# Checking and factoring FFN weights beside attention: sums on VectorE, checks in place, quarters copied DRAM to DRAM, weights fetched an item ahead

## The chip, the cores and the metric

The kernel runs on one core of a Trainium2 chip. The metric is the device time of one execution in microseconds. Three runs of the kernel before gave 885.43, 882.48 and 884.47 us, median 884.47. The engines are called as in the profile: PE is TensorE, PEld its weight load, DVE is VectorE, ACT is ScalarE, POOL is GpSimd and SP is SyncE, which here only issues DMAs.

## What is computed

`x` is (2, 2048, 256) in float32. The result is `x` plus causal attention plus a feed-forward network (FFN), both of the layernormed `x`:

```python
xn = layernorm(x)
q, k, v = xn @ Wq, xn @ Wk, xn @ Wv
attn = softmax(causal(q @ k.T) / 16) @ v @ Wo
tlin = lambda t, w, s: (t @ w.T) * s          # w holds only -1, 0 and 1
h = silu(tlin(xn, w1, s1)) * tlin(xn, w2, s2) # 256 -> 1024
h = gelu(tlin(h, h1, t1))                     # 1024 -> 1024
h = gelu(tlin(h, h2, t2))                     # 1024 -> 1024
out = x + attn + tlin(h, w3, s3)              # 1024 -> 256
```

The weights that setup_inputs makes are ternary, but the kernel does not take this for granted. It looks at them on the chip while attention runs and then branches.

## The kernel before, in words

**Stages.** Attention comes first (to about 285.6 us of the profiled execution), then the FFN (to about 875 us). Rows of `x` are worked in 8 blocks of 512 (4 to each batch). Every operand of attention's matmuls is held as a rounded high part and a low part, `hi` cast by ACT and `lo = src - hi` by DVE (`hi_lo`, L214 and L215).

**Attention.** `start_keys` normalizes a block (DVE statistics L238 and L239, ACT's square root L243, POOL's multiply and add L283). For the first batch PE transposes it (`ptx`, L309), for the second it goes through DRAM (`turn_keys`, L301 to L303). `weights_product` multiplies the weights ahead (`wqk` from `raw_q` and `raw_k`, `wvo` from `raw_v` and `raw_o`; L223 and L228). `score` (L349) makes one row tile of scores: matmuls L364, mask L370, eviction by DVE with a running maximum (L373), Exp by ACT (L385). Weights of the softmax have to be transposed for the next product. `turn_blocks` transposes 32 x 32 blocks on DVE and stores them to DRAM (`d`, L260), `fetch_blocks` reads them back in four quarters in the right order (`e`, L267), both on SP's queue. `turn` (L409) then casts `hi` by ACT (L423) and subtracts `lo` (L425) on POOL for odd blocks and on DVE for even ones. `weigh` (L434) multiplies by v (L443 and L448), scales (ACT L458, DVE L462) and stores `r_d` (L467).

**The work on FFN weights beside it.** One list, `looks` (L506), holds pairs of a gap and a function. `beside(cost)` is called for every piece of attention with the piece's cost in PE columns. From step 3 on it takes the next function off the list once the columns since the last one reach the gap (L574 to L579). The tiles are fetched by DMAs on ACT's queue into `stgp`, a pool of two buffers of 128 x 1024 (L160). There are three kinds of items:

- `look` (w1, w2 and w3): POOL rounds a copy for the FFN (L131), DVE masks the low bits (L526), ACT sums them up (L528).
- `look_signs` (h2) calls `compare`: ACT writes Sign of the tile into a half of `sums` (L537), DVE compares the tile with it (`not_equal`, L539) and accumulates the differences.
- `look_and_factor` (h1): two fetches, two `compare`s, and then, since the FFN multiplies h1 and h2 by a scheme of seven products of half matrices, the sums of half tiles that the scheme needs. `sums_of_factors` makes four (L150, POOL), two at a time. `store_factors` writes them to DRAM in one DMA of 1 MB and the three plain quarters in three DMAs of 256 KB from the staged tiles (L153 to L156, all on SP's queue).

`sums` is the memory of `xh0`, the FFN's first input, which is loaded from `xT_d[0]` at the end of attention (L669). So `compare` and `sums_of_factors` write the same tile:

```python
sign = sums[:, ts(i, 2), :].rearrange("p a o -> p (a o)")
nc.scalar.activation(sign, t, AF.Sign)
nc.vector.scalar_tensor_tensor(
    sign, t, 1.0, sign.bitcast(F32), ALU.mult, ALU.not_equal, accum_out=seen())
```

When the list is empty, DVE reduces all the results (L663), PE sums them over partitions (`pf`, L665) and DVE writes `flag` (L666). Every engine loads the flag at the end of attention (L1028) and branches to `ffn_ternary` or to a general FFN (L1029).

**FFN.** `ffn_ternary` works on pairs of blocks: `first` (w1 and w2, matmuls L715, evictions ACT L720 and DVE L721, splits L698 and L699, sums L741 and L742), the products with h1 and h2 (L763), and w3 (L871). `make_h2` uses `sums_of_factors` and `store_factors` as well, for h2, inside the FFN.

**What sets the order.** The program text is not the order of the queues. The whole is built with a scheduler that orders the instructions of each engine by their dependencies. `tc.issue_after(marks[..])` keeps a look behind the last score eviction (on DVE) or the last Exp (on ACT) that was written before it. DMAs on the queues of SP and ACT signal their landing on eight shared semaphores, handed out in turn, so a DMA can wait for the older one that had its semaphore.

Of the kernel before, what the change touches and what calls it, by code (L numbers as in the profile page):

```python
# [9 lines left out]
F32 = mybir.dt.float32  # L10
# [3 lines left out]
U32 = mybir.dt.uint32  # L14
AF = mybir.ActivationFunctionType
ALU = mybir.AluOpType
# [4 lines left out]
P = 128  # L21
# [18 lines left out]
LOW_BITS = 0xFFF  # L40
# [22 lines left out]
def attn_ffn_kernel(  # L63
# [35 lines left out]
    nc = tc.nc  # L99
    B, S, D = x.shape  # L100
# [4 lines left out]
    HC = H // P  # L105
    SC = 1024
# [14 lines left out]
    HB = H // 2  # L121
    HK = HC // 2
    factors = {k: dram.tile([P, len(STEPS), HK, HB], F32, name=f"factors_{k}") for k in ("h1", "h2")}
# [5 lines left out]
    def rounded(dst, src):  # L129

        nc.gpsimd.tensor_scalar(dst, src, 1.0, 0.0, ALU.mult, ALU.add)  # L131
# [4 lines left out]
    def rows(n, t):  # L136
        return ds((n % NB) * TB + t * P, P)

    def sums_of_factors(sums, halves, which):

        (a11, a21), (a12, a22) = ((t[:, :HB], t[:, HB:]) for t in halves)
        done = sums.bitcast(F32) if sums.dtype == F32R else sums
        for i in which:
            x, y, op = (
                (a21, a22, ALU.add),
                (done[:, 0, :], a11, ALU.subtract),
                (a12, done[:, 1, :], ALU.subtract),
                (a11, a21, ALU.subtract),
            )[i]
            nc.gpsimd.tensor_tensor(sums[:, i, :], x, y, op)  # L150

    def store_factors(f, c, sums, halves):
        nc.sync.dma_start(out=f[:, 1:5, c, :], in_=sums)  # L153
        nc.sync.dma_start(out=f[:, 0, c, :], in_=halves[0][:, :HB])
        for i in range(2):
            nc.sync.dma_start(out=f[:, 5 + i, c, :], in_=halves[1][:, ts(i, HB)])  # L156

    with ExitStack() as actx:
        cp = actx.enter_context(tc.tile_pool(name="cp", bufs=1))
        stgp = actx.enter_context(tc.tile_pool(name="stgp", bufs=2))  # L160
# [186 lines left out]
        marks = {}  # L347
# [122 lines left out]
        def score_steps(n, t):  # L470
            order = list(range(n - n % NB, n + 1))
            return [
                (6 * (TB if m < n else (t + 1) * P), lambda m=m: score(n, t, m, order))
                for m in order
            ]
# [29 lines left out]
        looked = [0]  # L505
        looks = []  # L506

        def seen():
            looked[0] += 1
            return low_bits[:, looked[0] - 1 : looked[0]]  # L510

        def fetched_weights(src, into):
            t = stgp.tile([P, SC], F32, tag="stg", name=f"stg_{len(looks)}_{looked[0]}")
            nc.scalar.dma_start(out=t, in_=src)
            into.append(t)

        def look(src, dst):
            got = []

            def bits():  # L520
                (t,) = got
                if dst is not None:
                    rounded(dst, t)
                tb = t.bitcast(U32)
                with tc.issue_after(marks["DVE"]):
                    nc.vector.tensor_scalar(tb, tb, LOW_BITS, None, ALU.bitwise_and)  # L526
                with tc.issue_after(marks["ACT"]):
                    nc.scalar.activation(t, tb, AF.Copy, accum_out=seen())  # L528

            looks.extend([(6000, lambda: fetched_weights(src, got)), (9000, bits)])  # L530

        sums = xh0.rearrange("p c h t -> p (c h) t")

        def compare(t, i):
            sign = sums[:, ts(i, 2), :].rearrange("p a o -> p (a o)")
            with tc.issue_after(marks["ACT"]):
                nc.scalar.activation(sign, t, AF.Sign)  # L537
            with tc.issue_after(marks["DVE"]):
                nc.vector.scalar_tensor_tensor(  # L539
                    sign, t, 1.0, sign.bitcast(F32), ALU.mult, ALU.not_equal, accum_out=seen()  # L540
                )

        def look_signs(src):
            got = []
            looks.extend([
                (6000, lambda: fetched_weights(src, got)),
                (9000, lambda: compare(got[0], looked[0] % 2)),
            ])

        def look_and_factor(src, f, c):  # L550
            got = []
            looks.extend([
                (6000, lambda: fetched_weights(src[:, c, :], got)),
                (2000, lambda: fetched_weights(src[:, c + HK, :], got)),
                (8000, lambda: compare(got[0], 0)),
                (2500, lambda: compare(got[1], 1)),
                (3500, lambda: sums_of_factors(sums, got, (0, 1))),
                (4000, lambda: sums_of_factors(sums, got, (2, 3))),
                (4000, lambda: store_factors(f, c, sums.bitcast(F32), got)),
            ])  # L560

        for src, dst in ((w1, w1_sb), (w2, w2_sb)):
            for c in range(src.shape[1]):
                look(src[:, c, :], dst[:, c, :])
        for c in range(HK):
            look_and_factor(h1, factors["h1"], c)
            for k in (2 * c, 2 * c + 1):
                look_signs(h2[:, k, :])
        for c in range(0, HC, SC // D):
            look(w3[:, c : c + SC // D, :].rearrange("p c d -> p (c d)"), None)  # L570

        since = [0]

# [28 lines left out]
        tiles = [divmod(i, NT) for i in range(NB * NT - 1, -1, -1)]  # L602
# [39 lines left out]
        while until < len(tiles) - 1:  # L642
# [7 lines left out]
            a = []  # L650
            if j < len(tiles):
                a = score_steps(*tiles[j])
                if j == 0:
                    a = []
            a = a + extra.get(j, [])
# [15 lines left out]
    def ffn_ternary(actx):  # L671
# [154 lines left out]
        def make_h2(c):  # L826
            halves = []
            for k in (c, c + HK):
                t = stgp.tile([P, SC], F32, tag="stg", name=f"stgt_h2_{k}")
                nc.sync.dma_start(out=t, in_=h2[:, k, :])  # L830
                halves.append(t)
            sums = stgp.tile([P, 4, HB], F32, tag="sums", name=f"sums_h2_{c}", bufs=1)
            sums_of_factors(sums, halves, range(4))
            store_factors(factors["h2"], c, sums, halves)
# [240 lines left out]
```

## Time and profile before

| quantity | value |
|---|---|
| median of three runs | 884.47 us (882.48 to 885.43) |
| profiled execution | 885.32 us, of it the span 883.4 us |
| PE busy | 855.4 us (97%) |
| DVE, ACT, POOL busy | 621.6, 498.1, 258.4 us |
| SP's DMA queue, ACT's DMA queue | 149.07 MB, 12.58 MB |
| sums on POOL in attention (L150) | 16, of 1290 to 1524 ns mean by kind |
| Sign on ACT (L537), compare on DVE (L539) | 16 each, 1054 and 1374 ns mean |
| factor stores, h1: 1 MB; 256 KB | 4 landing in 8.6 us; 12 landing in 3.6 us (medians) |
| fetch of weights (512 KB, h1 and h2) | 16 landing in 6.3 us (median) |

A line of the engine timelines reads: start in the span, duration of the group, engine, line, operation, output and inputs, shape, how many, and in brackets the idle time of the engine just before with what ended it. Neighbouring instructions of one line are drawn together, so a group may overlap the next by a pipelined instruction. The number after a line's xcount in the page's groups is busy time and mean duration.

### The profile page before, as it was taken

Reading aid. Unit: us, or ns where it says so; the run is one execution under the profiler, and the core shown is the slowest. Engines: PE = TensorE matmul, PEld = TensorE weight load, DVE = VectorE, ACT = ScalarE, POOL = GpSimd, SP = SyncE. Lnnn points to the kernel's source line nnn. Section 1 sums busy time; section 2 is a strip of 40 time slices with the busy share of each in tenths; the row PEclk is TensorE's granted clock in tenths of the full one; section 3 lists DMA queues with packets and bytes.
Section 4 is the critical chain, followed back from the end, with each engine's and each line's share of the span. In section 5 each row is a group of like instructions: output and inputs, shape, how many; then the busy total and the mean of one; then the engine's idle time right before and its main releaser. Section 6 shows DMA issues by size and latency. Waiting matters only on the chain.

```text
span 883.4 us, 12258 instructions
## 1 busy us (share of the span) xinstructions
PE 855.4 (97%) x4280; PEld 721.5 (82%) x4280; DVE 621.6 (70%) x1111; ACT 498.1 (56%) x881; POOL 258.4 (29%) x192
## 2 busy tenths in 40 slices
PE   8999889999998999999999999999999999999996
PEld 5988678888887878788988888888888898888886
DVE  6698667787763896786497596559568648848663
ACT  3456545755544655677256576626657635657670
POOL 4012835323211384440133051024115011502401
PEclk9999999999999999999999999999999999999999
DMA  8676699987882979844434444433444443144412
GB/s 268 243 224 200 195 313 298 343 298 207 294 253 58 377 256 343 294 143 143 137 102 144 143 143 144 155 109 118 143 142 144 143 144 96 48 143 144 143 48 76
DMA packets 63989, 162.51 MB, mean 184 GB/s; under 512 B 6704, under 2 KB 36528, under 8 KB 54704
## 3 DMA queue, kind: packets, MB, share of 16 engines
q1 hardware_dynamic: 60176, 149.07, 50.3%
q10 hardware_dynamic: 3744, 12.58, 5.0%
q8 instruction: 36, 0.59, 0.3%
q14 instruction: 33, 0.27, 0.1%
HBM read 113.92 MB, written 47.71 MB: 183 GB/s over the span
## 4 chain that ended last, share of the span: by engine, by line
PE 61%; DMA 4%; DVE 1%; POOL 1%; issue 0%; SPq 0%; POOLq 0%; DVEq 0%
PE ps_h_X L763 26%; PE ps_h_Z L763 13%; PE ps_w_B L715 10%; PE ps_h_Y L763 7%; PE ps_y L871 6%; DMA xt<-in_attn_x 2%; DMA w_h_A<-factors_h 1%; POOL rt L861 1%; DMA rt<-r_d 0%; DVE f_w_B L742 0%; DVE h_B L699 0%; POOL f_w_B L741 0%; DMA out<-yt 0%; DVE yt L878 0%; DVE yt L877 0%
## 5 line engine op out<-in xcount | busy, mean ns | idle before, releaser
L364 PE MATMUL pss<-k,q 128*128 128x512 f32 (+3 forms) x480 | 109.6, 369 | 3.7 <-ACT q L214 2.4
L364 PEld LDWEIGHTS pss<-k,q 128*128 128x128 f32 x480 | 82.3, 190 | 17.2 <-ACT q L214 2.7
L763 PE MATMUL ps_h_X<-h_h_T,w_h_S 128*128 128x512 f32 x384 | 89.0, 389 | 0.0
L443 PE MATMUL po<-v,pT 128*128 128x512 f32 x272 | 80.4, 407 | 6.5 <-ACT pT L423 5.8
L763 PEld LDWEIGHTS ps_h_X<-h_h_T,w_h_S 128*128 128x128 f32 x384 | 72.1, 188 | 15.0
L861 POOL TENSOR_TENSOR rt<-rt,xt 128x1024 f32<-128x1024 f32 x8 | 19.2, 2400 | 218.7 <-DMA rt<-r_d 212.1
L425 POOL TENSOR_TENSOR pT<-e,pT 128x512 fp32r<-128x512 f32 (+3 forms) x30 | 36.9, 1230 | 116.5 <-ACT pT L423 78.7
L784 ACT ACTIVATE k_h_u<-k_h_u,h_s_sb 128x512 f32<-128x512 f32 x64 | 46.3, 723 | 40.9 <-DVE k_h_u L783 40.7
L720 ACT ACTIVATE f_w_B<-ps_w_B,w_s_sb 128x512 f32<-128x512 f32 x64 | 43.0, 684 | 42.5 <-PE ps_w_B L715 42.5
L871 PEld LDWEIGHTS ps_y<-w_sbt,h_h_B 128*128 128x128 f32 x512 | 62.0, 192 | 0.3
L871 PE MATMUL ps_y<-w_sbt,h_h_B 128*128 128x256 f32 x512 | 62.1, 283 | 0.0
L715 PE MATMUL ps_w_B<-xh,w_sb 128*128 128x512 f32 x256 | 59.7, 390 | 1.3 <-DVE r L462 1.3
L715 PE MATMUL ps_w_B<-xh1t,w_sb 128*128 128x512 f32 x256 | 60.7, 397 | 0.0
L443 PEld LDWEIGHTS po<-v,pT 128*128 128x128 f32 x272 | 48.1, 192 | 15.0 <-ACT pT L423 6.7
L763 PE MATMUL ps_h_Y<-h_h_B,w_h_A 128*128 128x512 f32 x256 | 59.5, 389 | 0.6 <-DMA w_h_A<-factors_h 0.6
L763 PE MATMUL ps_h_X<-h_h_T,w_h_A 128*128 128x512 f32 x256 | 59.3, 389 | 0.0
L715 PEld LDWEIGHTS ps_w_B<-xh1t,w_sb 128*128 128x128 f32 x256 | 48.1, 188 | 12.0 <-ACT f_w_B L720 0.4
L715 PEld LDWEIGHTS ps_w_B<-xh,w_sb 128*128 128x128 f32 x256 | 47.8, 188 | 11.4 <-issue 1.5
L763 PEld LDWEIGHTS ps_h_Y<-h_h_B,w_h_A 128*128 128x128 f32 x256 | 48.0, 188 | 10.9 <-issue 1.0
L741 POOL TENSOR_TENSOR k_h_u<-k_h_p,k_h_u 128x512 f32<-128x512 f32 x16 | 24.3, 1526 | 110.0 <-ACT h_h_B L698 97.6
L763 PEld LDWEIGHTS ps_h_X<-h_h_T,w_h_A 128*128 128x128 f32 x256 | 48.1, 188 | 10.0
L385 ACT ACTIVATE s<-s,low 128x1024 f32<-128x1024 f32 (+7 forms) x48 | 43.0, 897 | 21.9 <-DVE low L379 21.8
(139 smaller groups left out, 1869.9 us busy)
## 6 DMA issues: line engine op xcount, KB each, us to landing
w_h_S<-factors_h SPq DMA_DIRECT2D x32, 1024.0 KB, 4.8
w_h_A<-factors_h SPq DMA_DIRECT2D x24, 1024.0 KB, 4.9
d<-b SPq DMA_DIRECT2D x18, 512.0 KB, 3.5
e<-d SPq DMA_DIRECT2D x72, 128.0 KB, 4.0
xT_d<-k SPq DMA_DIRECT2D x8, 1024.0 KB, 5.3
stg<-in_ffn_h_w ACTq DMA_DIRECT2D x16, 512.0 KB, 6.3
x<-in_attn_x SPq DMA_DIRECT2D x16, 256.0 KB, 5.3
r_d<-r SPq DMA_DIRECT2D x8, 512.0 KB, 5.8
```

Of the source, the lines that this page charges most:

```text
L364: nc.tensor.matmul(out=ps[:, :w], lhsT=qs[n][:, c, a, ts(t, P)], rhs=ks[m][:, c, b, :w], start=(k == 0), stop=(m < n and k == 3 * DC - 1),)
L385: marks["ACT"] = nc.scalar.activation(st["s"][:, at], st["s"][:, at], AF.Exp, bias=low, accum_out=st["sums"][:, u // UK : u // UK + 1],).ins
L425: engine.tensor_tensor(lo, src, hi.bitcast(F32), ALU.subtract)
L443: nc.tensor.matmul(out=st["po"], lhsT=pT[:, 0, ts(j, P)], rhs=vs[m][:, j, :, :], start=(m == first and j == 0), stop=False,)
L715: nc.tensor.matmul(out=p, lhsT=w[:, c, ts(o, P)], rhs=xh[:, c, a, :], start=(c == 0 and a == 0), stop=(c == DC - 1 and a == 1),)
L720: nc.scalar.activation(f, p1, AF.Silu, scale=sc["w1"][:, o : o + 1])
L741: nc.gpsimd.tensor_tensor(B["B12"][i], B["B22"][i], B["B12"][i], ALU.subtract)
L763: nc.tensor.matmul(out=out[o], lhsT=w[:, c, ts(o, P)], rhs=sets[right][c][:, a, :], start=(start and c == 0 and a == 0), stop=(c == HK - 1 ...
L784: nc.scalar.activation(C[k][o], r[o] if r else banks[o], AF.Gelu, scale=s[:, at : at + 1])
L861: nc.gpsimd.tensor_tensor(rest, rest, xt, ALU.add)
L871: nc.tensor.matmul(out=ys[t][:, :D], lhsT=h[c][:, a, ts(t, P)], rhs=w3_sb[:, c, :], start=(c == 0 and a == 0), stop=(c == HC - 1 and a == 1),)
```

## The change

- `sums_of_factors` takes the engine as an argument. For h1 in attention it is DVE, and the four sums of an item are four entries of the list, each kept behind the last score eviction. In the FFN it stays on POOL.
- The ternary check of h1 and h2 (`odd`) works in the staged tile: ACT writes the tile's absolute value over it, and DVE computes `(t != 0) != t` in place, accumulating. `sums` is no longer written by checks.
- The sums of an h1 item now come ahead of its checks, as the checks destroy the tile.
- The three plain quarters of h1 are copied from the input in DRAM to `factors` in DRAM by three DMAs on ACT's queue, in place of three stores from the staged tiles on SP's. The 1 MB store of the sums stays on SP.
- Items stand in one list with their sources. An item is fetched ahead of the work on the one before it where both fit in the pool's two buffers. The gaps are new. The two w3 items are interleaved with h1's items 2 and 3.

In the built program the order of the queues follows from these and from the scheduler. The twelve copies read only inputs, and they stand near the head of ACT's queue: three ahead of the first square root, two ahead of `wf_wqk`, three ahead of the third square root, one ahead of the cast of `q_3`, one ahead of the fourth square root and two ahead of `wf_wvo`. The last item of h1 and the three items after it stand in attention's last part, and the flag is made ahead of the products for the last row tile but one. The order of the FFN is almost that of before.

```diff
--- before.py
+++ after.py
@@ -136,7 +136,7 @@
     def rows(n, t):
         return ds((n % NB) * TB + t * P, P)
 
-    def sums_of_factors(sums, halves, which):
+    def sums_of_factors(sums, halves, which, engine=nc.gpsimd):
 
         (a11, a21), (a12, a22) = ((t[:, :HB], t[:, HB:]) for t in halves)
         done = sums.bitcast(F32) if sums.dtype == F32R else sums
@@ -147,7 +147,7 @@
                 (a12, done[:, 1, :], ALU.subtract),
                 (a11, a21, ALU.subtract),
             )[i]
-            nc.gpsimd.tensor_tensor(sums[:, i, :], x, y, op)
+            engine.tensor_tensor(sums[:, i, :], x, y, op)
 
     def store_factors(f, c, sums, halves):
         nc.sync.dma_start(out=f[:, 1:5, c, :], in_=sums)
@@ -509,65 +509,91 @@
             looked[0] += 1
             return low_bits[:, looked[0] - 1 : looked[0]]
 
-        def fetched_weights(src, into):
-            t = stgp.tile([P, SC], F32, tag="stg", name=f"stg_{len(looks)}_{looked[0]}")
-            nc.scalar.dma_start(out=t, in_=src)
-            into.append(t)
-
-        def look(src, dst):
-            got = []
-
-            def bits():
-                (t,) = got
-                if dst is not None:
-                    rounded(dst, t)
-                tb = t.bitcast(U32)
-                with tc.issue_after(marks["DVE"]):
-                    nc.vector.tensor_scalar(tb, tb, LOW_BITS, None, ALU.bitwise_and)
-                with tc.issue_after(marks["ACT"]):
-                    nc.scalar.activation(t, tb, AF.Copy, accum_out=seen())
-
-            looks.extend([(6000, lambda: fetched_weights(src, got)), (9000, bits)])
-
-        sums = xh0.rearrange("p c h t -> p (c h) t")
-
-        def compare(t, i):
-            sign = sums[:, ts(i, 2), :].rearrange("p a o -> p (a o)")
+
+        items = []
+
+        def low(tiles, dst):
+            (t,) = tiles
+            if dst is not None:
+                rounded(dst, t)
+            tb = t.bitcast(U32)
+            with tc.issue_after(marks["DVE"]):
+                nc.vector.tensor_scalar(tb, tb, LOW_BITS, None, ALU.bitwise_and)
             with tc.issue_after(marks["ACT"]):
-                nc.scalar.activation(sign, t, AF.Sign)
+                nc.scalar.activation(t, tb, AF.Copy, accum_out=seen())
+
+        def odd(t):
+
+            with tc.issue_after(marks["ACT"]):
+                nc.scalar.activation(t, t, AF.Abs)
             with tc.issue_after(marks["DVE"]):
                 nc.vector.scalar_tensor_tensor(
-                    sign, t, 1.0, sign.bitcast(F32), ALU.mult, ALU.not_equal, accum_out=seen()
-                )
-
-        def look_signs(src):
-            got = []
-            looks.extend([
-                (6000, lambda: fetched_weights(src, got)),
-                (9000, lambda: compare(got[0], looked[0] % 2)),
-            ])
-
-        def look_and_factor(src, f, c):
-            got = []
-            looks.extend([
-                (6000, lambda: fetched_weights(src[:, c, :], got)),
-                (2000, lambda: fetched_weights(src[:, c + HK, :], got)),
-                (8000, lambda: compare(got[0], 0)),
-                (2500, lambda: compare(got[1], 1)),
-                (3500, lambda: sums_of_factors(sums, got, (0, 1))),
-                (4000, lambda: sums_of_factors(sums, got, (2, 3))),
-                (4000, lambda: store_factors(f, c, sums.bitcast(F32), got)),
-            ])
+                    t, t, 0.0, t, ALU.not_equal, ALU.not_equal, accum_out=seen()
+                )
+
+        sums = xh0.rearrange("p c h t -> p (c h) t")
+
+        def sum_up(tiles, i):
+            with tc.issue_after(marks["DVE"]):
+                sums_of_factors(sums, tiles, (i,), nc.vector)
+
+        def store_sums(f, c):
+            nc.sync.dma_start(out=f[:, 1:5, c, :], in_=sums.bitcast(F32))
+
+        def copy_factors(src, f, c):
+            nc.scalar.dma_start(out=f[:, 0, c, :], in_=src[:, c, :HB])
+            for i in range(2):
+                nc.scalar.dma_start(out=f[:, 5 + i, c, :], in_=src[:, c + HK, ts(i, HB)])
+
+        def item_low(src, dst):
+            items.append(([src], [(0, lambda t: low(t, dst))]))
+
+        def item_signs(src):
+            items.append(([src], [(0, lambda t: odd(t[0]))]))
+
+        def item_factors(src, f, c):
+            steps = [(0, lambda t: sum_up(t, 0))]
+            steps += [(2500, lambda t, i=i: sum_up(t, i)) for i in (1, 2, 3)]
+            steps += [
+                (1500, lambda t: store_sums(f, c)),
+                (1500, lambda t: odd(t[0])),
+                (3000, lambda t: odd(t[1])),
+                (3000, lambda t: copy_factors(src, f, c)),
+            ]
+            items.append(([src[:, c, :], src[:, c + HK, :]], steps))
 
         for src, dst in ((w1, w1_sb), (w2, w2_sb)):
             for c in range(src.shape[1]):
-                look(src[:, c, :], dst[:, c, :])
+                item_low(src[:, c, :], dst[:, c, :])
+        w3_at = list(range(0, HC, SC // D))
         for c in range(HK):
-            look_and_factor(h1, factors["h1"], c)
+            item_factors(h1, factors["h1"], c)
             for k in (2 * c, 2 * c + 1):
-                look_signs(h2[:, k, :])
-        for c in range(0, HC, SC // D):
-            look(w3[:, c : c + SC // D, :].rearrange("p c d -> p (c d)"), None)
+                item_signs(h2[:, k, :])
+            if c >= 2:
+                w = w3_at[c - 2]
+                item_low(w3[:, w : w + SC // D, :].rearrange("p c d -> p (c d)"), None)
+
+        def fetched_weights(i):
+            for src in items[i][0]:
+                t = stgp.tile([P, SC], F32, tag="stg", name=f"stg_{i}_{len(tiles_of[i])}")
+                nc.scalar.dma_start(out=t, in_=src)
+                tiles_of[i].append(t)
+
+
+
+        tiles_of = [[] for _ in items]
+        looks = [(0, lambda: fetched_weights(0))]
+        for i, (srcs, steps) in enumerate(items):
+            nxt = i + 1 < len(items) and len(srcs) + len(items[i + 1][0]) <= 2
+            if nxt:
+                looks.append((4000, lambda i=i: fetched_weights(i + 1)))
+            ahead = i > 0 and len(srcs) + len(items[i - 1][0]) <= 2
+            gap = (8000 if ahead else 11000) if nxt else 15000
+            looks.append((gap, lambda i=i, f=steps[0][1]: f(tiles_of[i])))
+            looks += [(gap, lambda i=i, f=f: f(tiles_of[i])) for gap, f in steps[1:]]
+            if not nxt and i + 1 < len(items):
+                looks.append((4000, lambda i=i: fetched_weights(i + 1)))
 
         since = [0]
 
```

## The prediction

> **What bounds the kernel now.** I read the busy line of the page first, then the TensorE timeline with its idle times, then what the other engines did at those moments, and last the stretches of 20 us.
>
> ```profile
> PE 855.4 (97%) x4280; PEld 721.5 (82%) x4280; DVE 621.6 (70%) x1111; ACT 498.1 (56%) x881; POOL 258.4 (29%) x192
> ```
>
> TensorE is busy 855.4 of 883.4 us, so 28 us is all that any change which leaves the matmuls alone can win. About 8 us of that lies behind the last matmul and 2.8 us in the FFN (2.19 us at 317.80, 0.61 us at 354.97). The rest is in attention. These are its large gaps on the TensorE timeline (start, duration, group, idle time before it and what ended it):
>
> ```profile
> 9.43 2.09 PE L309 MATMUL ptx<-ident,x 128*128 128x128 f32 x8 [1.24 <-POOL x L283]
> ...
> 106.66 1.19 PE L443 MATMUL po<-v,pT 128*128 128x512 f32 x4 [1.35 <-ACT pT L423]
> 109.10 0.74 PE L448 MATMUL po<-v,pT 128*128 128x256 f32 x4 [1.25 <-DVE pT L425]
> ...
> 128.29 1.22 PE L364 MATMUL pss<-k,q 128*128 128x512 f32 x2 [2.36 <-ACT q L214]
> 129.31 1.91 PE L443 MATMUL po<-v,pT 128*128 128x512 f32 x4
> ...
> 267.80 1.70 PE L443 MATMUL po<-v,pT 128*128 128x512 f32 x4 [3.36 <-ACT pT L423]
> ```
>
> Four gaps of over 1 us stand beside work of FFN weights or behind a fetch of scores. After the 2.36 us gap four L443 matmuls take 1.91 us; with no gap before them the same four take 1.09. In the stretches of 20 us (columns: stretch, length, busy time of PE, PEld, DVE, ACT and POOL, PEclk, DMA share, GB/s) see PE's time and PEclk:
>
> ```profile
> 0.00:20.00 20.00, 16.35 (x60) 9.91 (x61) 12.58 (x52) 6.51 (x14) 10.61 (x28) 0.91 0.79 254
> 20.00:40.00 20.00, 20.00 (x144) 18.67 (x143) 11.41 (x25) 9.05 (x15) 2.10 (x2) 1.00 0.79 279
> 100.00:120.00 20.00, 17.41 (x98) 14.89 (x98) 16.87 (x43) 13.29 (x25) 10.27 (x8) 1.00 1.01 282
> 120.00:140.00 20.00, 17.64 (x93) 15.20 (x92) 11.41 (x29) 10.58 (x20) 3.80 (x4) 0.91 1.02 317
> 260.00:280.00 20.00, 16.64 (x90) 14.25 (x89) 7.61 (x20) 8.49 (x17) 4.31 (x4) 0.91 0.40 120
> ```
>
> What the neighbours did at 106 to 109 and at 125 us, from the timelines of VectorE, GpSimd and ScalarE:
>
> ```profile
> 106.14 1.22 DVE L539 SCALAR_TENSOR_TENSOR xh<-stg,xh 128x1024 fp32r<-128x1024 f32 x1
> ...
> 107.29 1.76 DVE L425 TENSOR_TENSOR pT<-e,pT 128x512 fp32r<-128x512 f32 x1
> ```
> ```profile
> 108.45 1.74 POOL L150 TENSOR_TENSOR xh<-stg,xh 128x512 fp32r<-128x512 f32 x1
> ```
> ```profile
> 125.39 2.00 ACT L537 ACTIVATE xh<-stg 128x1024 fp32r<-128x1024 f32 x2 [1.30 <-DMA factors_h<-xh]
> ...
> 127.66 0.57 ACT L214 CAST q<-pq 128x512 fp32r<-128x512 f32 x1
> ```
>
> So the 1.25 us gap is a subtraction (L425) behind a check (L539), and the subtraction took 1.76 us beside GpSimd's sum where it takes 0.69 alone. The 2.36 us gap is a cast of q that stood behind two Signs, which had themselves waited 1.30 us until the store of the last sums had read `xh`, because Sign writes where the sums lie.
>
> **What the Trainium skill says.** "SBUF — State Buffer", section "Who interferes with whom": only the port pair shared by VectorE and GpSimd contends, as an exclusive lock. The trace agrees: L425 at 1.76 against 0.69 us, L539 at 2.24 (97.88 us, beside GpSimd's L425) against 1.22. "DMA: Bandwidth & Descriptors", section "Queues, rings and completion order": each DMA engine goes round between the queues that have work. The trace of before has two such queues, SP's and ACT's, and no copy from DRAM to DRAM, nor does the page price one. "TensorE: Matmul & The Clock Gate", section "Part 1: The HAM clock gate": recent idleness throttles the clock. The trace agrees (1.91 against 1.09, and PEclk 0.91 in the two stretches with the longest gaps).
>
> **The change, part by part.**
>
> *Sums from GpSimd to VectorE.* GpSimd loses 16 sums, four each of 1295, 1524, 1521 and 1290 ns, 22.5 us. VectorE gains 16 tensor_tensors of 128x512 with two SBUF operands. The nearest row (L425 on VectorE, alone) is 0.69 us: 11 us. VectorE is busy 16.9 of 20 us in the fullest stretch, with the old checks of 1374 ns mean instead of 1.22: without GpSimd's sums 16 x 0.15 = 2.4 us comes back. Net some 8.6 us more on VectorE over 200 us, no path in the mean, but each sum can stand ahead of a score eviction (L373) or an L425. At TensorE I credit the whole gap at 109.10, 1.25 us.
>
> *Checks in place.* 16 Signs (1054 ns) become 16 Abs of the same shape, 16 not_equals stay not_equals of the same shape; I price the pairs equal. What goes is the wait of Sign for the store: 5.7 us in three places on ScalarE, one of them the cause at 128.29. Credit 2.36 us, and the slow clock after it: four L443 +0.82, six 384-column L364 at 1.59 against 1.20 +0.39, and as much again in the L320 behind, together 1.6 us. At 106.66 a Sign of 1.04 us ran just ahead of the cast for which TensorE waited 1.35: Abs goes elsewhere in ScalarE's order, credit 1.0.
>
> *Copies instead of stores.* SP loses 12 stores of 256 KB from `stg` (L154, L156; 3.6 us each to land) and the waits for `stg` ahead of them (7.5 us at L154). ACT gains 12 issues of 0.33 us, 4 us of its sequencer. In the built order they do not stand where the source has them. They depend on nothing, and all twelve stand at the head of ACT's queue: three ahead of the first square root (`std_3`), two ahead of `wf_wqk`, three ahead of `std_1`, one ahead of the cast of `q_3`, three between it and `wf_wvo`. Nine of them wait for an older DMA, since eight completion semaphores are shared by both queues. So at the start ACT waits for landings, and 3.1 MB more is read and written while 5.07 MB is moved in 20 us at a DMA share of 0.79. The DMA engines reach 380 GB/s in their full slices there: 8.2 MB takes 21.6 us, so the start just holds them if a copy costs what a load costs. `std_3` needs x_3 (its last half arrives at 6.4 us, the first copies are issued at about 1.7 to 2.5 behind raw_q and raw_k): up to 0.3 us late. The k_3 cast at 11.45 stands behind raw_o, which waits for the third copy: with half of 380 GB/s from 5.8 us on (raw_k's landing) three copies of 262 KB need 4.1 us, and land at 10 to 11; raw_o was issued at 10.50 anyway. The cast is late by 0 to 1 us, later ones likewise. I take +1.5 us; bounds 0 and +8.5 (the slower rival). Below zero it can't be: no load is removed there.
>
> *An item fetched ahead, four sums one by one.* Checks no longer wait for their fetch (1.1 us of ScalarE's idle time, off the path). But a fetch into a two-buffer pool waits for the check that frees the buffer, and now does so on ACT's queue: ahead of casts of pT (three times in the last 45 us) with VectorE's check ending just before. Such a stall of about 1 us reaches TensorE where no scores are left to do. New stalls in 100 to 250 us: +2.0 in all; bounds 0 and +5 (five of the size 0.98 at 96.61).
>
> *The tail.* The last checks ran at 250 us; now the last item of h1 and the three after it lie in attention's last 45 us. SP's order changes too. For: the four quarters of the fetch that TensorE waits for at 267.80 are now issued together, and ahead of the store of r_6; before, two stood behind it (the last ten fetches took SP 10.55 us from 260.43), and scores now lie between the products there. Against: the load of `xh` for the FFN now waits on SP until the last 1 MB store of sums has read it (8.6 us to land), and behind it stand the fetches of e_7_1_0. Issued at about 248.4 it lands at 257; those fetches began at 254.4, so 2.6 us late, of which TensorE has 2.8 us of other products to hide in. I credit 1.0 of the 3.36 plus 1.5 us (L443 1.70, L448 1.05 at the slow clock); bounds -4 and +3.
>
> *FFN.* Its order is almost that of before. GpSimd runs four L741 before an L150, where L150 stood ahead of the fourth: this may shorten the 2.19 us at 317.80 (GpSimd's L741 at 317.82 ended 1.68 later). Credit 0.5; bounds 0 and -2.
>
> Sum: -1.25 -2.36 -1.6 -1.0 -1.0 -0.5 +1.5 +2.0 = -4.2 us. Against the profiled execution's 885.32 us (span 883.4, 1.9 around it) that is 881.1. The profiled run lies 0.85 above the median of 884.47, so at the median's level the same sum gives 880.3; I keep 881.1, and judge the cases' sides against the median.
>
> **The rivals.**
>
> *Gaps move (884.0).* The scheduler orders every engine anew, VectorE has 11 us more ahead of evictions, and the 6.2 us of gaps return elsewhere. For: gaps at 96.61 and 153.70 have no look near them. Against: two causes (the wait for a store, the shared port) disappear altogether. New waits then cost 5 instead of 2: 884.1.
>
> *The copies hold ACT's queue at the start (888.1), slower.* If a DRAM-to-DRAM copy runs at half a load's rate, three copies beside SP's loads take 8.3 us, not 4.1: raw_o is issued at 14 to 15, the k_3 cast slips from 11.45 by 3.4 us, and wf_wvo (19.35), behind the twelfth copy, comes at 25 to 28, 6 to 8.5 us late, with v's products and all that follow behind it. Start +8.5 instead of +1.5: 881.1 + 7.0 = 888.1. It decides from a copy rate below about 0.6 of a load's. For: nothing measures it here, and the start has a DMA share of 0.79 already. Against: the copies are behind the first four loads, and TensorE has scores of block 3 in hand at 18 us.
>
> *The tail clears too (875.8).* Whole tail 4.9 instead of 1.0, new waits 0.6 instead of 2.0: 881.1 - 3.9 - 1.4.
>
> **How the numbers follow.** A measurement here tells 0.3%, 2.65 us, from no change. Forecast (877 to 884): 0.45, of which 0.12 lies within 2.65 us. Gaps move: 0.18 (0.04 faster, 0.10 same, 0.04 slower). Copies: 0.25 (0.22 slower, 0.03 same). Tail clears: 0.12. Faster 0.49, same 0.25, slower 0.26. Range 875 to 889: from the tail's case to just above the copies'; since the cases lie on both sides, the forecast's own range stands beside it: 877 to 884.
>
> **What would show it.** Start: first twelve copies on ACT's queue before 20 us; wf_wvo within 2 us of 19.35 (forecast) or past 25 (rival). GpSimd idle of L150 before the FFN, VectorE's L425 at 0.69. No idle time of ScalarE on a store of sums; no 2.36 us gap near 128, PEclk 1.00 there. Tail: the gap at 267.80 under 2.5 us, SP waiting for the last store ahead of `xh`. Wrong if TensorE's idle before 30 us grows by over 3 us, if VectorE's sums end gaps at L364, or if the last 45 us hold more idle than 4.9 us.

## The result, and the profile after

| | before | changed |
|---|---|---|
| median of five executions | 884.47 us (882.48 to 886.63) | 877.43 us (876.67 to 878.56) |
| ratio, 95% interval | | 0.9924 [0.9899, 0.9949] |
| profiled execution (span) | 885.32 (883.4) | 877.43 (875.6) |
| attention ends, first FFN matmul | 285.62 us | 279.72 us |
| last group of matmuls (w3) starts | 859.92 us | 853.02 us |
| span after the last matmul ends | 8.0 us | 7.1 us |

The kernel became 0.76% faster. The forecast was 881.1, so the sign and the range held, and the size was short by 3.7 us. Of these, 0.85 is a matter of level: the forecast was counted down from the profiled 885.32, and the median lies 0.85 lower. Profile against profile, the forecast's sum of -4.2 stands against -7.9. Of the 7.8 us between the two spans, 5.9 had been won by the end of attention, 1.0 more by the last group of matmuls, and 0.9 after it.

The changed kernel's busy line:

```profile
PE 854.3 (98%) x4280; PEld 721.6 (82%) x4280; DVE 630.6 (72%) x1127; ACT 498.0 (57%) x881; POOL 235.6 (27%) x176
```

Its larger gaps on the TensorE timeline:

```profile
9.36 1.52 PE L309 MATMUL ptx<-ident,x 128*128 128x128 f32 x6 [1.62 <-POOL x L283]
...
22.55 0.50 PE L364 MATMUL pss<-k,q 128*128 128x512 f32 x1 [0.63 <-ACT k L214]
...
123.43 0.73 PE L364 MATMUL pss<-k,q 128*128 128x512 f32 x2 [0.44 <-ACT q L214]
125.98 0.50 PE L364 MATMUL pss<-k,q 128*128 128x512 f32 x1 [1.71 <-DVE q L215]
...
215.69 1.20 PE L443 MATMUL po<-v,pT 128*128 128x512 f32 x4 [1.05 <-DVE r L462]
261.27 1.20 PE L443 MATMUL po<-v,pT 128*128 128x512 f32 x4 [1.93 <-ACT pT L423]
263.60 1.22 PE L448 MATMUL po<-v,pT 128*128 128x256 f32 x4 [1.13 <-DVE pT L425]
```

And its stretches (columns as in the prediction):

```profile
0.00:20.00 20.00, 16.30 (x56) 9.82 (x57) 11.89 (x49) 5.24 (x11) 8.70 (x25) 0.83 0.89 297
20.00:40.00 20.00, 19.37 (x142) 17.86 (x141) 12.78 (x26) 8.99 (x16) 3.86 (x6) 1.00 1.03 385
100.00:120.00 20.00, 20.00 (x111) 17.12 (x110) 18.75 (x37) 12.10 (x24) 7.12 (x5) 1.00 1.00 299
120.00:140.00 20.00, 17.85 (x96) 15.27 (x96) 14.61 (x38) 9.84 (x20) 2.57 (x2) 0.91 1.01 296
260.00:280.00 20.00, 16.31 (x85) 13.71 (x86) 9.01 (x17) 8.00 (x16) 3.78 (x3) 0.91 0.19 50
```

Adding up the gaps of each timeline: those before 50 us (without the first 1.19) went from 2.45 to 3.29, those from 50 to 240 us from 8.49 to 3.20, those from 240 us to the FFN from 3.36 to 3.06, those inside the FFN from 2.80 to 2.01 (the 1.28 us ahead of the FFN's first matmul is the same in both). TensorE's busy time fell by 1.1 us besides. Most of the win is in the middle of attention. The start became dearer, and the stretch from 120 to 140 us still holds its gap and its slow clock.

### The profile page after: what moved, and what is told of

Same layout as the page of the kernel before. It is cut to its first block, busy times and chain, and to the rows that moved or that the text cites. A ratio compares the mean times of both kernels' runs of the same rounds, so it can differ in the third digit from the quotient of the medians.

```text
span 875.6 us, 12225 instructions
## 1 busy us (share of the span) xinstructions
PE 854.3 (98%) x4280; PEld 721.6 (82%) x4280; DVE 630.6 (72%) x1127; ACT 498.0 (57%) x881; POOL 235.6 (27%) x176
## 4 chain that ended last, share of the span: by engine, by line
PE 70%; DMA 13%; DVE 7%; issue 2%; ACT 2%; SPq 2%; POOL 2%; ACTq 0%; DVEq 0%; POOLq 0%
PE ps_h_X L789 26%; PE ps_w_B L741 13%; PE ps_h_Z L789 13%; PE ps_h_Y L789 7%; PE ps_y L897 6%; DMA e<-d 6%; DMA d<-b 4%; DMA stg<-in_ffn_h_w 2%; SPq L267 2%; DVE b L255 2%; PE pv L336 1%; PE po L443 1%; DVE stg L530 1%; POOL x L283 1%; DVE s L373 1%
## 5 line engine op out<-in xcount | busy, mean ns | idle before, releaser
L364 PE MATMUL pss<-k,q 128*128 128x512 f32 (+3 forms) x480 | 111.0, 369 | 3.1 <-DVE q L215 1.7
L364 PEld LDWEIGHTS pss<-k,q 128*128 128x128 f32 x480 | 81.8, 189 | 16.2 <-DVE q L215 2.1
L425 POOL TENSOR_TENSOR pT<-e,pT 128x512 fp32r<-128x512 f32 (+3 forms) x30 | 36.3, 1212 | 162.3 <-ACT pT L423 101.6
L423 ACT CAST pT<-e 128x512 fp32r<-128x512 f32 (+3 forms) x60 | 32.6, 573 | 49.6 <-DMA e<-d 38.3
L741 PEld LDWEIGHTS ps_w_B<-xh1t,w_sb 128*128 128x128 f32 x256 | 48.1, 188 | 11.8
```

The source lines that it names most:

```text
L364: nc.tensor.matmul(out=ps[:, :w], lhsT=qs[n][:, c, a, ts(t, P)], rhs=ks[m][:, c, b, :w], start=(k == 0), stop=(m < n and k == 3 * DC - 1),)
L423: nc.scalar.copy(hi, src)
L425: engine.tensor_tensor(lo, src, hi.bitcast(F32), ALU.subtract)
L741: nc.tensor.matmul(out=p, lhsT=w[:, c, ts(o, P)], rhs=xh[:, c, a, :], start=(c == 0 and a == 0), stop=(c == DC - 1 and a == 1),)
```

## The experiments

Twelve kernels ran, in three sets, each with executions of the kernel before beside it (medians 884.70, 884.76 and 885.16); the five executions of the changed kernel stand apart from these sets. The intervals are some 0.2% wide to each side, so smaller differences between two rows are not told apart. Single executions of one kernel spread over several us (52 of the kernel before ran from 880.04 to 889.97), so verdicts go by the ratios, and a profile shows one execution. The last column is TensorE's idle time in the stretch from 90 to 170 us, 80 minus its busy time there.

| kernel | median, us | ratio to before, 95% interval | idle 90 to 170 us |
|---|---|---|---|
| before | 884.47 | 1 | 7.30 |
| changed | 877.43 | 0.9924 [0.9899, 0.9949] | 2.15 |
| b_dve | 882.96 | 0.9974 [0.9955, 0.9993] | 5.03 |
| b_copy | 879.07 | 0.9939 [0.9922, 0.9955] | 5.14 |
| b_inplace | 885.59 | 1.0002 [0.9982, 1.0021] | 9.17 |
| a_tied | 887.02 | 1.0015 [0.9994, 1.0035] | 6.91 |
| a_mid | 880.95 | 0.9953 [0.9936, 0.9971] | 4.17 |
| a_store | 878.95 | 0.9947 [0.9927, 0.9966] | 3.58 |
| a_pool | 880.24 | 0.9954 [0.9938, 0.9969] | 3.56 |
| a_noahead | 878.93 | 0.9940 [0.9922, 0.9957] | 5.61 |
| b_null | 883.31 | 0.9989 [0.9971, 1.0007] | 7.70 |
| a_null | 878.85 | 0.9931 [0.9907, 0.9955] | 4.21 |
| b_poolq | 899.90 | 1.0167 [1.0135, 1.0199] | 13.19 |
| a_poolq | 887.71 | 1.0032 [1.0017, 1.0047] | 5.36 |

The theory at first was that of the prediction: what pays is that look work no longer stands beside attention's casts and subtractions. Its main rival was that SP's queue pays.

### One part alone: b_dve

```diff
-                (3500, lambda: sums_of_factors(sums, got, (0, 1))),
-                (4000, lambda: sums_of_factors(sums, got, (2, 3))),
+                (3500, lambda: sum_up(got, 0)),
+                (2000, lambda: sum_up(got, 1)),
...
+            with tc.issue_after(marks["DVE"]):
+                sums_of_factors(sums, tiles, (i,), nc.vector)
```

> The kernel before with one part alone: h1's four sums per item on VectorE, one by one. Theory (the gain comes from work that stood beside attention's casts and subtractions: the shared port and the wait of Sign for the store of sums): the port is free of GpSimd's sums, so the 1.25 us gap at 109 goes, VectorE pays 15 us in pieces of 0.7 to 1.2: 1 to 3 us faster, 881.5 to 883.5 (median before 884.47). Rival A (the gain comes from SP's queue, which loses twelve stores): no change, 884 to 885. Rival B (a new order of the queues, whatever the part): anything between 880 and 888, with gaps in new places that no row of sums explains.

It gave 0.26% [0.07, 0.45], some 2.3 us: as the theory expected in size, but not in place. The gap at 109 did not go. In b_dve's profile it is 2.05 us, at 111.20, and what stands ahead of the subtraction on VectorE is the check, stretched from 1.22 to 2.32 us:

```profile
108.21 2.32 DVE L539 SCALAR_TENSOR_TENSOR xh<-stg,xh 128x1024 fp32r<-128x1024 f32 x1
...
110.47 0.68 DVE L425 TENSOR_TENSOR pT<-e,pT 128x512 fp32r<-128x512 f32 x1
```

GpSimd ran nothing but attention's own L425 then (1.28 us from 108.17). So GpSimd's sums were not alone in stretching the work of VectorE. In this profile the last matmul ends 4.5 us earlier than in the kernel before (870.97 against 875.43), and 3.7 of them are lost behind it, where 11.7 us pass instead of 8.0. The end of the kernel varies that much, so one profile does not tell what the part is worth.

### One part alone: b_copy

```diff
-                (4000, lambda: store_factors(f, c, sums.bitcast(F32), got)),
+                (4000, lambda: store_and_copy(src, f, c)),
...
+            nc.scalar.dma_start(out=f[:, 0, c, :], in_=src[:, c, :HB])
+            for i in range(2):
+                nc.scalar.dma_start(out=f[:, 5 + i, c, :], in_=src[:, c + HK, ts(i, HB)])
```

> The kernel before with one part alone: the three plain quarters of h1 copied from DRAM to DRAM on ACT's queue, in place of twelve stores on SP's. The copies stand at the head of ACT's queue as in the changed kernel. Theory: the start costs 1.5 to 2 us, SP's relief gives back 0 to 1 us, so 884.5 to 886.5. Rival A (SP's relief is the gain): 3 to 5 us faster, 879.5 to 881.5, with the waits of L423 for e<-d shorter from 90 us on.

0.61% faster, 5.4 us: the rival was right on this part and the theory wrong. The start cost what it costs in the changed kernel (gaps of 3.26 us before 50 us). What came back can be followed at one place. In the kernel before, the store of a plain quarter (L154) stood on SP's queue for 5.3 us, until its tile had landed, and a fetch of scores stood behind it. ScalarE's cast L423 then waited 4.45 us for that fetch, VectorE's subtraction and an eviction (L373) came late after it, and TensorE stood for 0.98 us. The kernel before, on SP's queue (a group's duration holds the waits inside it), ScalarE and TensorE:

```profile
80.91 1.27 SPq L267 DMA_DIRECT2D e<-d  x2
87.52 0.34 SPq L154 DMA_DIRECT2D factors_h<-stg  x1
...
88.43 11.89 SPq L267 DMA_DIRECT2D e<-d  x7
```
```profile
94.02 0.62 ACT L423 CAST pT<-e 128x512 fp32r<-128x512 f32 x1 [4.45 <-DMA e<-d]
```
```profile
96.61 1.66 PE L364 MATMUL pss<-k,q 128*128 128x512 f32 x6 [0.98 <-DVE s L373]
```

And b_copy, SP's queue and ScalarE:

```profile
87.68 12.48 SPq L267 DMA_DIRECT2D e<-d  x9
```
```profile
91.64 0.62 ACT L423 CAST pT<-e 128x512 fp32r<-128x512 f32 x1 [1.34 <-DMA e<-d]
```

The cast runs 2.4 us earlier and TensorE has no gap there. At 45 us it was 1.9 us behind the kernel before, at 96.6 us it is level, and without the gap of 1.35 us at 106.66 it is 1.2 us ahead. This is one place in one profile, and not a rule: b_null keeps the stores, holds SP for 5.0 us at L154 and has no gap near 97. Nor does the sum of such waits tell the gain. Between 30 and 290 us L423 waited 36.3 us for fetches of `e` in the kernel before and 26.8 in b_copy, but 38.3 in the changed kernel, and 20.2 in b_dve and 21.0 in a_store, which leave the stores on SP. So b_copy shows that the edit pays, and for the most of it not by which wait. In the tail the 3.36 us gap became 1.08 and 0.45. The gap of 1.25 us behind VectorE's L425 (107.87) stayed, with L425 at 1.76 us beside GpSimd, as in the kernel before.

### One part alone: b_inplace

```diff
-                nc.scalar.activation(sign, t, AF.Sign)
+                nc.scalar.activation(t, t, AF.Abs)
...
-                    sign, t, 1.0, sign.bitcast(F32), ALU.mult, ALU.not_equal, accum_out=seen()
+                    t, t, 0.0, t, ALU.not_equal, ALU.not_equal, accum_out=seen()
```

The sums and stores of an h1 item also move ahead of its two checks.

> The kernel before with one part alone: checks in place (Abs over the tile, not_equal over it), so that the sums and the stores of an item's quarters come ahead of its checks. Theory: ScalarE no longer waits for the store of sums (5.7 us in three places), so 1 to 3 us faster, 881.5 to 883.5; but Abs on h1's tiles now has to wait until the three 256 KB stores have read them (3.6 us each to land), which may give it all back. Rival A: no change, 884 to 885. If this wait is what the copies are for: slower by 1 to 3 us, 885.5 to 887.5, with L537 waiting for factors_h<-stg.

No change, so the theory missed. The waits for the store of sums are gone from ScalarE, but no wait of Abs for a 256 KB store came instead. Another did: a fetch of weights, held on ScalarE's queue, and behind it stood what TensorE needed. ScalarE:

```profile
148.16 0.33 ACTq L514 DMA_DIRECT2D stg<-in_ffn_h_w  x1
148.60 0.47 ACT L458 ACTIVATE y<-po,inv 128x256 f32<-128x256 f32 x1 [5.36 <-DMA x<-d_x]
...
151.96 1.12 ACT L301 CAST k<-x 128x512 fp32r<-128x512 f32 x2
```

and TensorE:

```profile
152.61 1.22 PE L320 MATMUL pq<-k,wqk 128*128 128x512 f32 x2 [6.44 <-ACT k L301]
```

The scaling L458 does not read `x`. In the built order the fetch ahead of it waits for a completion semaphore that a fetch of `x` on SP's queue had before it. Until that `x` landed, ScalarE stood for 5.36 us and then still had a check to run ahead of the cast of k.

### Where the copies stand: a_tied and a_mid

```diff
+            with tc.issue_after(marks["ACT"]):
+                nc.scalar.dma_start(out=f[:, 0, c, :], in_=src[:, c, :HB])
```

a_tied, in the first set, is this edit for all three copies of an item. After that set theory 2 took the place of the theory: what pays is that the bytes and issues of the quarters leave SP's queue in attention's full stretch. a_mid, in the second set, has the edit too, and calls `copy_factors` for one item at each of steps 1 to 4, not from the list.

> The changed kernel with one edit: each item's three copies are kept behind the last Exp that was written before them, so that they are issued in attention at about 110, 150, 185 and 240 us and not at the head of ACT's queue. Theory (the start costs 1.7 us by the gaps before 46 us): 875.5 to 876.5 against 877.43. Rival C (in attention, where the DMA share is 1.0 from 100 to 160 us, the copies delay the fetches of e and stand in ACT's queue ahead of casts): 878 to 881, and the start's gain is given back.

> The changed kernel with the copies moved on purpose: each item's three copies stand behind an Exp of steps 1 to 4, at about 40 to 60 us, past the crowded start and ahead of the stretch in which the DMA share is 1.0. Theory 2, formed after the last four runs (what pays is that 3.1 MB are no longer moved by SP's queue in the stretch from 100 to 260 us; where they go before it is a matter of the start's 1.7 us): 875 to 877, the start's gaps as in the kernel before. Rival B (each edit draws a new order, and the changed kernel has drawn a good one): 878 to 886, with gaps at new places between 100 and 270 us though the DMA engines are as free there as in the changed kernel.

a_tied lost everything: 887.02 against 877.43, on the side of rival C and past its numbers. Its start is that of the kernel before (gaps of 2.40 us before 50 us), but in attention the queue of ScalarE was held as in b_inplace. ScalarE, then TensorE:

```profile
162.00 0.34 ACTq L581 DMA_DIRECT2D stg<-in_ffn_h_w  x1
162.38 0.47 ACT L458 ACTIVATE y<-po,inv 128x256 f32<-128x256 f32 x1 [3.31 <-DMA factors_h<-xh]
```
```profile
163.43 1.19 PE L443 MATMUL po<-v,pT 128*128 128x512 f32 x4 [2.30 <-DVE r L462]
```

The 1 MB store (issued at 153.91) had the semaphore for which the fetch waits in the built order. The scaling, VectorE's L462 and TensorE stood behind. a_mid, with the copies at 40 to 60 us, kept 0.47%. It missed its forecast of 875 to 877 and lies within the range of its rival B. The start's gaps were saved (1.89 us), but the tail of the profile holds 5.03 us, 3.50 in one gap. So the kernel is slower with the copies in attention's full stretch (0.9% over the changed kernel) than with them at 40 to 60 us (0.3%), and the hoist to the head of the queue, which I had counted as pure cost, is not beaten by either later place. Whether a_tied lost by the copies' bytes or by the waits that they put on ScalarE's queue, these runs do not separate.

### One part taken out: a_store, a_pool, a_noahead

```diff
-                (1500, lambda t: store_sums(f, c)),
+                (1500, lambda t: store_factors(f, c, sums.bitcast(F32), t)),
```
```diff
-                sums_of_factors(sums, tiles, (i,), nc.vector)
+                sums_of_factors(sums, tiles, (i,))
```
```diff
-            nxt = i + 1 < len(items) and len(srcs) + len(items[i + 1][0]) <= 2
+            nxt = False
```

a_store also drops the copies from the list, a_pool the hold of the sums behind the last eviction, and a_noahead has the old gaps (6000 and 9000).

> The changed kernel without its copies: the three quarters are stored from the staged tiles on SP's queue, after the 1 MB store of the sums and ahead of the checks that overwrite the tiles. Theory 2: the gain is gone or turned, since the bytes are back in attention and Abs waits for the stores to have read its tile: 883 to 888. Rival A2 (sums on VectorE and the fetch an item ahead carry the gain, copies not needed): 876 to 879.

> The changed kernel with h1's sums on GpSimd again, still one by one. If VectorE's sums are worth what they gave alone (0.26% of the kernel before, 1 to 4 us by the interval): 878.5 to 881. Rival (with copies out of attention the port matters no more, and VectorE saves 15 us of sums): 876 to 878.

> The changed kernel without the fetch an item ahead, with the gaps of the kernel before (6000 columns ahead of a fetch, 9000 ahead of its work). Fetches no longer stand in ACT's queue behind a check that has to free the buffer, and checks may wait for a fetch (3.5 us in two places now). Expected, as fetches land in 6 us and 9000 columns are about 4.5 us of TensorE: within 2 us of the changed kernel, 876 to 880. Rival B (order): up to 885 with gaps at places that no fetch explains.

Each of the three keeps 0.46 to 0.60%. a_store went against theory 2: without any copy, with the stores on SP in attention, the kernel is still 0.53% faster than before. Abs waited 0.8 us in all for a store that reads its tile. a_pool and a_noahead came as expected. Single parts add up to 0.85% (0.26, 0.61 and -0.02), the whole is 0.76%, and no part that is taken out costs more than 0.3%. This reads as if the parts reach for the same idle time, but it is not shown: the intervals of all three overlap with that of the changed kernel, and a_store and a_noahead (878.95 and 878.93) stand no higher than a_null below (878.85), in which no part is missing. What stays open is how a_store comes by its 0.53%: it has the sums on VectorE, the checks in place behind the stores and the fetch ahead all at once, and no run separates these three from each other in the absence of copies.

### Two controls: b_null and a_null

```diff
-            looks.extend([(6000, lambda: fetched_weights(src, got)), (9000, bits)])
+            looks.extend([(6000, lambda: fetched_weights(src, got)), (8000, bits)])
```
```diff
-        looks = [(0, lambda: fetched_weights(0))]
+        looks = [(4000, lambda: fetched_weights(0))]
```

> A control: the kernel before with one number changed, the gap between a fetch of w1, w2 or w3 and its work, 8000 columns for 9000. No work is removed, added or moved to another engine; later looks come some 1000 columns earlier. Theory 3 (what an edit of the looks gives is for a good part the order that it draws; a fetch of weights on ACT's queue waits for an older DMA that had the same completion semaphore, and casts stand behind it, at places that shift with every edit): the time moves by 1 to 5 us either way, 880 to 888, with the large gaps at other places than before. Theory 2 (the parts themselves carry the gain): 884 to 885.5.

> The same control on the changed kernel: the first fetch comes 4000 columns later and the list with it, nothing else. Theory 3: 877 to 885, with large gaps elsewhere. Theory 2: 877 to 878.5.

Neither control is clear of the kernel that it was made from, so no shift of the order is seen to give anything like the 5 to 7 us of b_copy and the changed kernel. Theory 3 is not refuted for small moves: both medians (1.2 us under that of the kernel before, or 1.9 under that of their set, and 1.4 us over that of the changed kernel) lie in its ranges and just outside those of theory 2. A new order does move the gaps. In b_null's profile one of 5.06 us stands at 132.45, where the kernel before has none, behind a cast that waited 7.80 us for a fetch of scores. SP had drawn out the issues of that fetch and the one before it over 8.19 us. TensorE, then SP's queue:

```profile
132.45 2.08 PE L443 MATMUL po<-v,pT 128*128 128x512 f32 x4 [5.06 <-ACT pT L423]
```
```profile
118.78 8.19 SPq L267 DMA_DIRECT2D e<-d  x8
```

But their sum hardly changes (7.70 against 7.30 us of idle time from 90 to 170 us). In the changed kernel it does: a_null's profile, the slowest of its seven executions, has 4.21 us there against 2.15, and 5.78 against 3.20 from 50 to 240 us. So the place of a gap is drawn anew with each order, and how much of the sum is drawn with it stays open.

### Fetches on GpSimd's queue: b_poolq and a_poolq

```diff
-                nc.scalar.dma_start(out=t, in_=src)
+                nc.gpsimd.dma_start(out=t, in_=src)
```

> The kernel before with the fetches of looks issued by GpSimd's queue in place of ACT's. If casts and scalings that stand behind a waiting fetch on ACT make the gaps, these go: 879 to 882. If instead GpSimd's own waits (L425 stands behind a fetch that waits for its buffer) make new ones, or its issue takes more than ACT's 0.33 us: 884 to 888.

> The changed kernel with the fetches of looks issued by GpSimd's queue, which has lost its sums and so stands idle for longer; the copies stay on ACT's. Theory 3: the stalls of ACT behind fetches go, 875 to 877.5, a little faster than the changed kernel. Else, with new waits of GpSimd's L425 behind fetches that wait for a check: 878 to 882.

Both are slower than the kernel before and past all their forecasts. New waits came on GpSimd in b_poolq (total, times, longest):

```profile
POOL stg L514 <- DVE xh L539: 38.5, 5, 12.6
```

A fetch into a two-buffer pool waits for the check that frees its buffer, and on GpSimd attention's own work then stands behind it. But only one gap of TensorE, 1.07 us, ends with GpSimd's L425. The four gaps over 2 us that b_poolq has in attention (4.41, 5.59, 2.02 and 2.89 us) end with casts of ScalarE. Ahead of the first, at 110.25, a check on ScalarE had waited for a fetch that GpSimd issued only at 101.49, after its own L283 and L425:

```profile
107.51 1.06 ACT L537 ACTIVATE xh<-stg 128x1024 fp32r<-128x1024 f32 x1 [6.07 <-DMA stg<-in_ffn_h_w]
```

So the waits run both ways, and which of them costs the 1.7% is not shown. Taking the shared semaphores from ScalarE was to test the mechanism of b_inplace and a_tied; since another wait took its place, these two runs do not tell how much of the whole it explains.

## Why the prediction was right and where it was short

**Start, +1.5: right.** Gaps before 50 us rose by 0.84 us, PEclk in the first 20 us fell from 0.91 to 0.83, and the group of 24 L364 that begins at 43.93 in the kernel before begins at 45.65, 1.72 later. The gaps are half of it, and the rest goes with the slower clock. Ten of the twelve copies waited for an older DMA, where I had counted nine. The copies cost what loads cost; the issue row and two lines of ScalarE's timeline in the changed kernel:

```profile
factors_h<-in_ffn_h_w ACTq DMA_DIRECT2D x12, 256.0 KB, 5.8
```
```profile
20.97 0.38 ACT L228 ACTIVATE wf_wvo<-ps_wvo 128x256 f32<-128x256 f32 x1 [2.22 <-issue]
...
21.92 1.07 ACT L214 CAST k<-ptx 128x512 fp32r<-128x512 f32 x2
```

`wf_wvo` is 1.6 us late, within the 2 that I had set as the mark; the slower rival needed it past 25. Its premise, a copy at half a load's rate, did not hold: full slices of the start moved 370 to 410 GB/s.

**The gap at 128.29, -2.36, and the slow clock after it, -1.6: failed.** The wait of Sign for the store did go. In its place Abs waits for its fetch, and on VectorE the check and a transpose stand ahead of the low part of q:

```profile
121.48 1.06 ACT L528 ACTIVATE stg<-stg 128x1024 f32<-128x1024 f32 x1 [1.75 <-DMA stg<-in_ffn_h_w]
...
122.80 0.57 ACT L214 CAST q<-pq 128x512 fp32r<-128x512 f32 x1
```
```profile
122.58 1.23 DVE L530 SCALAR_TENSOR_TENSOR stg<-stg 128x1024 f32<-128x1024 f32 x1 [2.11 <-ACT stg L528]
...
123.73 1.24 DVE L255 STREAM_TRANSPOSE b_x<-x 128x1024 f32<-128x1024 f32 x1
...
125.25 0.68 DVE L215 TENSOR_TENSOR q<-pq,q 128x512 fp32r<-128x512 f32 x1
```

0.44 and 1.71 us remain of 2.36, and PEclk is 0.91 again. The step from "the wait for the store goes" to "the whole gap goes" left out what stands next in the two queues: on ScalarE the fetch of the checked tile, on VectorE the check itself. The statement that checks no longer wait for their fetch failed with it: these waits rose from 1.1 to 3.5 us. The 1.6 us for the clock was too large as well. Its third term, 0.39 us, was put on the L320 behind, but those twelve took 2.98 us at 132.79 and 2.92 at 78.76 and 188.18 in the kernel before, so they were not slow.

**The gaps at 106.66 and 109.10, -1.0 and -1.25: gone in the changed kernel, but not for the reasons given.** With GpSimd's sums gone but the checks as they were (b_dve) both are larger (1.82 and 2.05 us). With the copies alone the first goes, though a Sign still runs just ahead of its cast, and the second stays. That both credits came true in the changed kernel is in part luck.

**New waits, +2.0: the mis-sized term.** I expected the uncredited gaps to stay and new ones to come. From 50 to 240 us the gaps that I had credited were 4.96 us, the others (0.98 at 96.61, 0.71 at 153.70 and smaller ones) 3.53. Of the whole only 3.20 is left, so this stretch gave 5.3 us, where my steps for it, without the clock, say 4.6 less 2.0. b_copy names a term that I had priced at nothing: SP's twelve stores. I had written down that they and their 7.5 us of waits for `stg` leave SP's queue, and drew no gain from it. The gap of 0.98 us at 96.61, of which I said that no look is near it, stands at the end of just such a wait. b_copy measures 5.4 us for the part, its cost at the start paid. That the same term carries the changed kernel is not shown, since a_store keeps 0.53% without it.

**VectorE's sums, 11 us: too cheap.** Their means are 1219, 947, 893 and 702 ns, 15.0 us in all, where I took 0.69 each, and the check's mean is 1360 against 1374 ns, so the 2.4 us did not come back: GpSimd's L425 stretches a check as its sums did (2.32 us in b_dve). VectorE's L425 takes 781 ns in the mean, from 854, and not the 0.69 us that I had named as a sign. No gap on TensorE's timeline in the changed kernel ends behind a sum.

**Tail, -1.0: nearly nothing.** 3.06 us of gaps for 3.36, with PEclk 0.91 in both. SP did wait for the last 1 MB store ahead of the load of `xh` (2.1 us), from 241 to 243 us, in time for the fetches behind it.

**FFN, -0.5: right in sign.** 2.80 to 2.01 us of gaps. The end of the kernel gave 0.9 us more that no step had. No run was made for it, and over the fourteen profiles the stretch behind the last matmul takes 7.1 to 11.8 us, so it may be chance.

## What to carry to other kernels

Look at the in-order queue in which side work stands, and not only at the engine time that it costs: here, taking twelve small stores off the queue of the critical fetches gave 0.6% as a single edit, and moving 22 us of sums to a faster engine 0.3%. In this program a DMA issued from a compute engine's queue is a wait of that engine, for its buffer and for whatever older DMA had its completion semaphore (5.36 us in b_inplace, 3.31 in a_tied), so look at what stands behind it. And where several parts aim at one idle stretch, price the stretch and not the parts, and run a control that only shifts the order before believing in any one gap.

## What the runs showed of the hardware that I had not expected

Copies from DRAM to DRAM of 256 KB with rows of 2 KB land in 5.8 us (median of 12) in a stretch that moves about 380 GB/s, as raw_v and raw_o do there (5.6 us each). And a VectorE instruction with one SBUF input seems to be held by GpSimd too: in a_poolq the mask of low bits, 0.70 us in the mean of the changed kernel, took 3.66 us and ended at 101.73. GpSimd ran L283 and L425 back to back from 93.73 to 101.18. TensorE waited 1.78 us for the eviction behind it.

```profile
98.07 3.66 DVE L521 TENSOR_SCALAR stg<-stg 128x1024 uint32<-128x1024 uint32 x1
...
101.65 0.68 DVE L373 TENSOR_SCALAR_CACHE_REDUCE s<-pss 128x512 f32<-128x512 f32 x1
```
